# Beginning the six steps of the second layer's factors one pair later in the middle stage

## Chip, cores and metric

The kernel runs on one core of one Trainium2 chip. The metric is device time in microseconds for one launch, the median of three runs. Every number below that has a decimal point is microseconds unless it says otherwise.

## What is computed

The input `x` has 32 sequences of 64 channels and 1024 positions. Two layers follow each other. Each one adds to `x` a product of a convolution stack with a feed-forward matrix:

```python
x = x + ffn0(cond0(x, style))     # then the same with cond1 and ffn1

def _layer(x, style, w, b, mw, mb, typ):          # four of them in a cond
    s = style @ mw.T + mb                         # one scale per sequence and channel
    weight = SCALE * w * s[:, None, :, None]
    demod = lax.rsqrt(jnp.sum(weight * weight, axis=(2, 3)) + EPS)
    weight = weight * demod[:, :, None, None]
    ...                                           # conv: same, up + blur, same, blur + down

# ffn0: scores = x @ Wr.T; top 16 of 64 experts, softmax -> G
#       h = einsum('nd,krd->nkr', x, A); out = 2 * einsum('nkr,kdr->nd', h * G, B)
# ffn1: W[i,o] = scales[o] * nibble[i,o] - zeros[o]; out = x @ W + bias
```

`s`, `demod` and the small matrices made from them and from the convolution weights do not depend on `x`. They are the *factors* of a layer.

## The kernel before

The 128 partitions hold two sequences of 64 channels each, a *pair*; there are `NP = 16` pairs. The program has three stages in time. In the first (0 to 402) every pair goes through the first layer's convolutions and through the product with the scores and `A`; the gated result goes to DRAM (`hgd`). In the middle stage (402 to 628) every pair's result is loaded again (`hg`), transposed on TensorE, and multiplied with `B`; the residual is added and the new `x` goes to DRAM in two forms (`x1d`, `x1e`). In the last stage (628 to 905) every pair goes through the second layer's convolutions and the product with the unpacked weights.

The change lies in the middle stage, in a loop over the pair `p`. One turn of it for a pair from the third on (the first two pairs, `WHOLE`, are simpler and also split `B` into parts):

- `turned_h(p + 1)` transposes the next pair's `hg` with 8 instructions on TensorE into two PSUM banks (`ht`, L1021). VectorE cuts off the high bits (`hh`, L148) and subtracts them (`tlh`, L859), ScalarE copies the high part (`thh`, L863) and scales the low part (`tlh`, L867). GpSimd forms the difference of the two (`tdh`, L875) in `crossed`.
- `layer0b(p)` multiplies: 16 instructions with `thh`, 16 with `tlh` (together called Q here) and 16 with `tdh` (called D), all L895, for two halves of 512 columns with two PSUM banks each. Four banks (`fps`) is all there is, so the next pair's Q begins in a bank that this pair has given up.
- VectorE joins the banks with the residual: L1065 and L1066 for the first half, L1065 and L1066 for the second. Then it makes the differences `dd` (L1108, L1110), beside small edge copies on ScalarE (L1109, L1113) and GpSimd (L1107, L1117), and the SP queue writes them out (L1102, L1104, L1114), loads the next residual (L1047) and the `hg` of two pairs on (L1009).

Beside this the loop makes the second layer's factors. `factors(1, ...)` is a generator of six steps, and one `next(set1)` per pair runs one of them:

1. the loads: `mw`, `mb` on the SP queue (L192, L194), `cw`, `b`, `cu` on ScalarE's queue (L193, L195, L196);
2. squares of the weights on VectorE (L206, L207, L209), copies of the weights on ScalarE (L214 to L220), the styles on TensorE (`sps`, L226, four calls that issue 8 matmuls) with L230 to L233 on VectorE, and a chain on GpSimd that composes a blur with a convolution kernel: two memsets (L238, L239), copies, six additions (L246), copies into `iw` and `cu` (L253, L259);
3. the sums for `demod` on TensorE (`dps`, L263), the root on ScalarE (L271), the reciprocal on VectorE (L272), three transposes (`w2t`, L279) with four copies (L282 to L285), and the first `rows` transpose (L339);
4. about fifteen small instructions on VectorE (L294 to L314) and two on ScalarE;
5. a first constant column on TensorE (`cs`, L325) with two instructions on VectorE (L327, L328);
6. a second one, the second `rows` transpose, and the DMA of the rows to DRAM (`rowd`, L332), from which the tables `tbl` of the last stage are loaded (L563).

Their scratch lies in the array `cv`, where the unsplit `B` was before and where two inputs of the last stage (`cv<-x1e`, L666) and zeroed columns (`clear`, `clear_y`) come after. The order on each engine is made by a scheduler from the order of the program. It lets an instruction move ahead where its data permit; `tc.issue_after(v)` holds what is inside until `v` has been issued. The steps stand behind the pair's `tdh` in this way (`done["td"]`).

Of the kernel before, what the change touches and what calls it, by code (L numbers as in the profile page):

```python
# [62 lines left out]
def adaln_ffn_kernel(ctx: ExitStack, tc: tile.TileContext, t, out: bass.AP):  # L63
# [65 lines left out]
    def yv(n):  # L129
        o = O_Y + (n % 2) * Y  # L130
        return cv[:, o : o + Y]
# [229 lines left out]
    def split_weights(raw, w, ks, into, name, crossed=True):  # L361

        for k in ks:
            ws = block(k, [P, 3, w], F32R, f"{name}{k}")
            for c in range(0, w, H):
                cs = slice(c, min(c + H, w))
                h = high(raw[k][:, cs], f"{name}h{k}_{c}")
                nc.gpsimd.tensor_tensor(ws[:, 1, cs], raw[k][:, cs], h, ALU.subtract)  # L368
                nc.scalar.copy(ws[:, 0, cs], h)  # L369
            into[k] = ws  # L370
            if crossed:
                crossed_weights(into, k)
# [34 lines left out]
    def load_q():  # L407
        qw = wk.tile([P, L], I32, tag="w4", name="qw", bufs=3)
        nc.sync.dma_start(qw, t["qweight"])
        return qw  # L410

    def unpacked(qw):


        wq = []
        aux = block(3, [P, 3, L], F32, "aux")
        for n, v in enumerate(("scales", "zeros", "bias")):
            nc.sync.dma_start(aux[:, n], t[v].partition_broadcast(P))
        for j in range(PACK):
            if j % 3 == 0:  # L420
                w = block(j // 3, [P, 3, QW], F32R, f"wq{j}")
            v = w[:, j % 3]
            nc.gpsimd.memset(v[:, 0:1].bitcast(F32), 1.0)
            nc.gpsimd.memset(v[:, 1:2].bitcast(F32), 0.0)
            for c in range(2):
                nib = wk.tile([P, H], I32, tag="hi", name=f"nib{j}_{c}", bufs=3)
                with tc.issue_after(done["dd"].ins):
                    nc.vector.tensor_scalar(
                        nib,
                        qw[:, c * H : (c + 1) * H],  # L430
                        4 * j,
                        15,
                        ALU.logical_shift_right,
                        ALU.bitwise_and,
                    )
                nc.scalar.copy(v[:, 2 + c * H : 2 + (c + 1) * H], nib)
            wq.append(v)
            if j % 3 == 2:
                yield
        yield wq, aux  # L440
# [204 lines left out]
    def clear(i):  # L645

        for n in range(2):
            if i == 0:
                nc.gpsimd.memset(xdv(n)[:, 0 : L + 3 : L + 2], 0.0)
            nc.gpsimd.memset(fwv(n)[C:, NT * C : 8 * C], 0.0)  # L650

    def clear_y(ys):
        for y in ys:
            nc.gpsimd.memset(y[:, YO : YO + HQ + 1 : HQ], 0.0)
# [216 lines left out]
    def crossed(key):  # L871

        if key in toks and len(toks[key]) == 2:
            td = tokens("td", f"td{key}")
            done["td"] = nc.gpsimd.tensor_tensor(  # L875
                *(v.rearrange("p a b -> p (a b)") for v in (td, *toks[key])), ALU.subtract
            )
            toks[key].append(td)
# [128 lines left out]
    def load_h(p):  # L1007
        hg = wk.tile([P, L], F32, tag="w4", name=f"hg{p}", bufs=3)
        nc.sync.dma_start(hg, hgd[p])  # L1009
        return hg  # L1010

    def turned_h(p, hg):
        whole = p in WHOLE
        key = f"h{p}"
        th = tokens("th", f"th{key}", F32 if whole else F32R)
        toks[key] = [th] if whole else [th, tokens("tl", f"tl{key}")]
        for g in range(2):
            ps = cpst(f"ht{p}_{g}")
            for c in range(4):
                k = 4 * g + c  # L1020
                nc.tensor.transpose(  # L1021
                    ps[:, c * P : (c + 1) * P], hg[:, k * P : (k + 1) * P], ident
                )
            ks = slice(4 * g, 4 * g + 4)

            def d(v):
                return v[:, ks].rearrange("p a b -> p (a b)")

            if whole:
                nc.scalar.copy(d(th), ps)  # L1030
            else:
                split(ps, lambda v: v, d(th), d(toks[key][1]), f"hh{p}_{g}")
        if not whole:
            scaled_low(toks[key][1])
# [3 lines left out]
    def load_residual(p):  # L1038
        if p in WHOLE:
            v = tokens("tl", f"xres{p}", F32).rearrange("p a b -> p (a b)")  # L1040
        elif p < NP - 1:
            v = cv[:, O_Y + Y : O_Y + Y + L]
        elif p < NP:
            v = wk.tile([P, L], F32, tag="w4", name="xres", bufs=3)
        else:
            return
        nc.sync.dma_start(v, t["x"][p])  # L1047
        residual[p] = v
# [137 lines left out]
    def load(k, h=None, rooms=(None, None)):  # L1186
        if k < len(todo):
            i, p = todo[k]
            for h in range(2) if h is None else (h,):
                xin.setdefault(k, []).append(load_x(i, 2 * p + h, rooms[h]))  # L1190

    def tables_of(k):
        if k < len(todo):
            tables(*todo[k])

    def outer_of(k):
        if k < len(todo):
            outer_outputs(*todo[k])

    def begin(k, hs=range(2)):  # L1200
        if k < len(todo):
            i, p = todo[k]
            for h in hs:
                if k < DIRECT:
                    n = 2 * p + h
                    room = xev(n) if k != 1 else room4[:, 2 * XD + 2 * h * HQ :]
                    xin[k][h] = scaled_positions(n, room, *xin[k][h])
                elif i == 0:
                    differences(2 * p + h, *xin[k][h])
                else:  # L1210
                    modulated(2 * p + h)

    def compose(k):
        if k < len(todo):
            gs[k] = composed1(*todo[k])

    def conv(k, h):
        if k < len(todo):
            i, n = todo[k][0], 2 * todo[k][1] + h
            ys.setdefault(k, []).append(first(i, n, yv(n), xin[k][h]))  # L1220
            if i == 1:
                load(k + 1, h)

    def weights(k):
        if k < len(todo):
            fw[k] = composed2(*todo[k], gs.pop(k))

    def later(k, h):
        if k < len(todo):
            i, p = todo[k]  # L1230
            rest(i, 2 * p + h, ys[k][h], fw[k][h])

    def run(g):
        for _ in g:
            pass
# [117 lines left out]
    for p in range(NP):  # L1353
        if p + 1 < NP:
            turned_h(p + 1, hg)
        if p + 2 < NP:
            hg = load_h(p + 2)
        if p == NP - 1:
            clear_y([yv(1)])
            conv(NP, 1)  # L1360
            tables_of(NP + 2)
            outer_of(NP + 1)
            begin(NP + 1)
        if p <= len(WHOLE):
            load_residual(p)
        main = layer0b(p, braw if p in WHOLE else wb)
        next(main)
        if p in WHOLE:
            split_weights(braw, L, range(4 * p, 4 * p + 4), wb, "wb")
        if p == 7:  # L1370
            clear(1)
            clear_y([yv(0)])
        if p == LAST:
            load(NP)
            tables_of(NP)
            set_ends = ends(1, 0, LAST, cv[:, O_FW:])
        if p in (LAST, LAST + 1):
            next(set_ends)
        if p == NP - 2:
            qw = load_q()  # L1380
            tables_of(NP + 1)
            outer_of(NP)
            begin(NP)
            compose(NP)
            conv(NP, 0)
            weights(NP)
        if p == NP - 1:
            unpacking = unpacked(qw)
            compose(NP + 1)
            next(unpacking)  # L1390
            later(NP, 0)
            next(main)
            next(unpacking)
            conv(NP + 1, 0)
            next(main)
            later(NP, 1)
            second = next(unpacking)
            weights(NP + 1)
            next(main)
            conv(NP + 1, 1)  # L1400
        next(main, None)
        if p in (LAST, LAST + 1):
            next(set_ends)
        run(main)
        if p + 1 < NP:
            crossed(f"h{p + 1}")
        if 0 < p < 7:
            with tc.issue_after(done["td"].ins):
                next(set1, None)
        if p == LAST + 1:  # L1410
            run(set_ends)
            for n in range(2):
                nc.gpsimd.memset(fwv(n)[C:, NT * C : 8 * C], 0.0)
# [71 lines left out]
```

## Time and profile before

| quantity | value |
|---|---|
| median of 3 runs | 908.75 (907.94 to 909.59) |
| the profiled execution | 906.81 |
| its span | 904.7 |
| mean granted TensorE clock in it | 0.999 of full speed |
| busy: TensorE, VectorE, GpSimd, ScalarE | 97%, 78%, 52%, 36% of the span |

The span runs from the first to the last instruction in the profile; 2.1 of the profiled execution's time lie outside it. Times of instructions below count from the span's start. Matmul ends are modelled, so the distance from one start to the next is what a group of matmuls costs; a bracket at the end of a row gives the idle time before it and what ended that.

### The profile page before, as it was taken

Reading aid. Unit: us, or ns where it says so; the run is one execution under the profiler, and the core shown is the slowest. Engines: PE = TensorE matmul, PEld = TensorE weight load, DVE = VectorE, ACT = ScalarE, POOL = GpSimd, SP = SyncE. Lnnn points to the kernel's source line nnn. Section 1 sums busy time; section 2 is a strip of 40 time slices with the busy share of each in tenths; the row PEclk is TensorE's granted clock in tenths of the full one; section 3 lists DMA queues with packets and bytes.
Section 4 is the critical chain, followed back from the end, with each engine's and each line's share of the span. In section 5 each row is a group of like instructions: output and inputs, shape, how many; then the busy total and the mean of one; then the engine's idle time right before and its main releaser. Section 6 shows DMA issues by size and latency. Waiting matters only on the chain.

```text
span 904.7 us, 14847 instructions
## 1 busy us (share of the span) xinstructions
PE 876.4 (97%) x5133; PEld 786.2 (87%) x5133; DVE 709.2 (78%) x1450; ACT 328.9 (36%) x717; POOL 468.2 (52%) x605
## 2 busy tenths in 40 slices
PE   5989999999999999999899999999999999999997
PEld 4877789999999999994688888788899999999997
DVE  4565888888888888577986666669998899999986
ACT  6435433333333344333332221247233323333230
POOL 7325654444444444456572222433776767676674
PEclk9999999999999999999999999999999999999999
DMA  8521232222222221354476665556433243333321
GB/s 252 138 72 53 54 95 71 83 79 77 77 77 77 76 77 71 106 175 154 136 227 209 212 195 159 181 191 187 148 111 112 89 130 113 110 109 118 120 65 70
DMA packets 49738, 109.81 MB, mean 121 GB/s; under 512 B 13700, under 2 KB 22400, under 8 KB 49664
## 3 DMA queue, kind: packets, MB, share of 16 engines
q1 hardware_dynamic: 48704, 107.88, 38.9%
q10 hardware_dynamic: 960, 0.99, 0.4%
q8 instruction: 41, 0.67, 0.3%
q14 instruction: 33, 0.27, 0.1%
HBM read 70.97 MB, written 37.88 MB: 120 GB/s over the span
## 4 chain that ended last, share of the span: by engine, by line
PE 77%; DVE 11%; issue 4%; POOL 4%; DMA 2%; ACT 1%; ACTq 0%; SPq 0%; DVEq 0%; POOLq 0%
PE h L895 18%; PE o L895 15%; PE q L1146 12%; PE f L611 6%; PE r L784 6%; PE r L815 5%; PE c L735 5%; PE r L792 3%; PE g L588 3%; PE c L730 2%; DMA x1e<-dd 1%; PE ht L1021 1%; DVE x L1066 1%; POOL wa L368 1%; POOL tdh L875 1%
## 5 line engine op out<-in xcount | busy, mean ns | idle before, releaser
L700 POOL TENSOR_TENSOR cv<-cv 128x256 f32<-128x256 f32 x120 | 77.8, 649 | 123.5 <-DVE su L938 72.7
L697 DVE TENSOR_TENSOR cv<-cv 128x257 f32<-128x257 f32 x120 | 99.8, 863 | 1.2 <-ACT cv L720 1.0
L732 ACT ACTIVATE yt<-c,be,al 128x257 f32<-128x257 f32 x56 | 31.7, 566 | 120.1 <-PE c L730 108.9
L1146 PE MATMUL q<-wq,thx 128*128 128x342 f32 x384 | 73.0, 332 | 1.6 <-ACT thx L853 1.6
L634 POOL TENSOR_TENSOR cv<-cv 128x256 f32<-128x256 f32 x60 | 55.0, 917 | 33.9 <-ACT cv L629 33.9
L1146 PE MATMUL q<-wq,tlx 128*128 128x342 f32 x384 | 72.4, 330 | 0.0
L895 PE MATMUL h<-wa,tdx 128*128 128x352 f32 (+1 forms) x336 | 72.1, 351 | 0.2 <-DVE wa L376 0.2
L800 DVE TENSOR_TENSOR rt<-r,tbl 128x256 f32<-128x256 f32 x60 | 25.0, 417 | 56.3 <-PE r L792 56.3
L611 PE MATMUL f<-gs,iw 128*128 128x128 f32 (+1 forms) x384 | 68.1, 327 | 0.0
L784 PE MATMUL r<-cv 128*128 128x128 f32 x480 | 66.6, 282 | 0.9 <-POOL cv L634 0.5
L611 PEld LDWEIGHTS f<-gs,iw 128*128 128x128 f32 x384 | 61.9, 190 | 5.5
L784 PEld LDWEIGHTS r<-cv 128*128 128x128 f32 x480 | 63.6, 196 | 3.0 <-POOL cv L634 1.7
L875 POOL TENSOR_TENSOR tdx<-thx,tlx 128x1024 fp32r<-128x1024 f32 x14 | 35.5, 2536 | 57.6 <-ACT tlx L867 48.1
L895 PE MATMUL h<-wa,thx 128*128 128x352 f32 (+1 forms) x336 | 64.7, 333 | 0.0
L1146 PEld LDWEIGHTS q<-wq,thx 128*128 128x128 f32 x384 | 60.3, 189 | 3.6 <-ACT thx L853 2.7
L815 PE MATMUL r<-cv 128*128 128x128 f32 x480 | 63.4, 274 | 0.0
L1146 PEld LDWEIGHTS q<-wq,tlx 128*128 128x128 f32 x384 | 61.9, 189 | 0.8
L895 PE MATMUL h<-wa,tlx 128*128 128x352 f32 (+1 forms) x336 | 62.4, 327 | 0.0
L895 PE MATMUL o<-wb,thh 128*128 128x512 f32 x224 | 59.9, 400 | 2.6 <-ACT wb L369 1.6
L626 ACT COPY cv<-f 128x256 f32<-128x256 f32 x64 | 24.0, 375 | 100.8 <-PE f L611 90.3
L895 PEld LDWEIGHTS h<-wa,tdx 128*128 128x128 f32 x336 | 57.1, 188 | 2.3 <-DVE wa L376 0.5
L815 PEld LDWEIGHTS r<-cv 128*128 128x128 f32 x480 | 58.3, 191 | 0.0
(306 smaller groups left out, 2128.6 us busy)
## 6 DMA issues: line engine op xcount, KB each, us to landing
cv<-in_x_dram SPq DMA_DIRECT2D x60, 256.0 KB
cv<-x1e SPq DMA_DIRECT2D x64, 192.5 KB
x1e<-dd SPq DMA_DIRECT2D x16, 514.0 KB
hgd<-hs SPq DMA_DIRECT2D x16, 512.0 KB
hg<-hgd SPq DMA_DIRECT2D x16, 512.0 KB
x1d<-x SPq DMA_DIRECT2D x16, 512.0 KB
xb<-x1d SPq DMA_DIRECT2D x16, 512.0 KB
out_dram<-o SPq DMA_DIRECT2D x15, 512.0 KB
```

The costliest lines, as they stand in the source:

```text
L588: nc.tensor.matmul(ps[:, k * P : (k + 2) * P], tw[:, k].rearrange("p a b -> p (a b)"), r.rearrange("p a b c -> p (a b c)"), start=(k == 0) ...
L611: done["f"] = nc.tensor.matmul(pv[:, n : n + 2 - k], iw[:, e].rearrange("p a b -> p (a b)"), v, start=(m == 0), stop=(m == len(steps) - 1) ...
L634: nc.gpsimd.tensor_tensor(f[:, 4 * P : 6 * P].rearrange("p (a b) -> p a b", b=P), v[:, :, 0], v[:, :, 1], ALU.add,)
L697: nc.vector.tensor_tensor(d[:, k], yo[:, k : k + HQ], yb, ALU.subtract)
L700: nc.gpsimd.tensor_tensor(e[:, :, k], d[:, :, 2 * k : 2 * k + HQ - 2 : 2], d[:, :, 1 : HQ - 1 : 2], ALU.subtract)
L732: nc.scalar.activation(yt, mid, AF.Identity, bias=be0[:, n : n + 1], scale=a)
L735: done["c"] = nc.tensor.matmul(ps, w[:, q], xe[:, o : o + w_], start=True, stop=True)
L784: nc.tensor.matmul(ps[:, j * P : (j + 1) * P], y[:, j + k : j + k + 2 * P - 1 : 2], w(4 + k), start=(k == 0), stop=(k == 1),)
L815: done["r"] = nc.tensor.matmul(ps[:, j * P : (j + 1) * P], y[:, YE + (2 * q + k) * P : YE + (2 * q + k + 1) * P], w(q + 2 * k), start=True ...
L875: done["td"] = nc.gpsimd.tensor_tensor(*(v.rearrange("p a b -> p (a b)") for v in (td, *toks[key])), ALU.subtract)
L895: nc.tensor.matmul(banks[l == 2], toks[key][l][:, order(k)], w[:, cols], start=(k == first and l != 1), stop=(k == last and l in (2, min(n ...
L1146: nc.tensor.matmul(ps, half[:, k], wq[at(k)][:, c * QC : (c + 1) * QC], start=(k == 0 and j == 0), stop=(k == NC - 1 and j == 1),)
```

## The change

`next(set1)` is called in the turns of pairs 2 to 7 where it was called in those of pairs 1 to 6, and the zeroing that shares the scratch is called in pair 8's turn, not in pair 7's. Nothing is added or left out.

```diff
@@ -1367,7 +1367,7 @@
         next(main)
         if p in WHOLE:
             split_weights(braw, L, range(4 * p, 4 * p + 4), wb, "wb")
-        if p == 7:
+        if p == 8:
             clear(1)
             clear_y([yv(0)])
         if p == LAST:
@@ -1404,7 +1404,7 @@
         run(main)
         if p + 1 < NP:
             crossed(f"h{p + 1}")
-        if 0 < p < 7:
+        if 1 < p < 8:
             with tc.issue_after(done["td"].ins):
                 next(set1, None)
         if p == LAST + 1:
```

The order of instructions per engine, set side by side for the two programs, has the same instructions on every engine. Step 1's ten loads, the squares of step 2 on VectorE (L206, L207, L209) and its copies on ScalarE (L214 to L220) stand in the same place in both: the scheduler had already carried them ahead, and the zeroing too, except L654. The rest of the steps stands one pair later on each engine.

## The prediction

> **What bounds the kernel now.** I read the page first, for the bound of the whole.
>
> ```profile
> PE 876.4 (97%) x5133; PEld 786.2 (87%) x5133; DVE 709.2 (78%) x1450; ACT 328.9 (36%) x717; POOL 468.2 (52%) x605
> PE 77%; DVE 11%; issue 4%; POOL 4%; DMA 2%; ACT 1%; ACTq 0%; SPq 0%; DVEq 0%; POOLq 0%
> ```
>
> TensorE is busy for 97% of the span and makes up 77% of the chain that ended last. So a moved instruction counts if it changes how long TensorE idles, or if it leaves a place where TensorE idled anyway. The second view is the timeline of TensorE in the middle stage; pairs 3 and 4 of it are here.
>
> ```profile
> 443.02 3.79 PE L895 MATMUL o<-wb,tdh 128*128 128x512 f32 x16
> 446.65 0.97 PE L226 MATMUL sps<-condT,cv 128*128 128x32 f32 x8
> 447.45 1.07 PE L1021 MATMUL ht<-ident,hg 128*128 128x128 f32 x8
> 449.56 2.08 PE L895 MATMUL o<-wb,thh 128*128 128x512 f32 x8 [1.04 <-DVE cv L1065]
> ...
> 456.94 3.79 PE L895 MATMUL o<-wb,tdh 128*128 128x512 f32 x16
> 460.57 0.97 PE L263 MATMUL dps<-cv 128*128 128x32 f32 x8
> 461.37 0.53 PE L279 MATMUL w2t<-ident,cw 128*128 128x128 f32 x3
> 461.73 1.04 PE L1021 MATMUL ht<-ident,hg 128*128 128x128 f32 x8
> ...
> 470.30 3.79 PE L895 MATMUL o<-wb,tdh 128*128 128x512 f32 x16
> ```
>
> The row to see is the fourth. Pair 3's first product starts after 1.04 of idle, released by VectorE's L1065. Just before it stand `sps`, which is moved, and the transposes. From there to pair 8 TensorE idles once more, for 0.54 before the second `rows` transpose at 501.04. A pair with no step beside it takes 11.79 from one start to the next (511.53 to 523.32).
>
> The third view is VectorE's timeline, to see what L1065 was late for.
>
> ```profile
> 447.46 0.68 DVE L859 TENSOR_TENSOR tlh<-ht,hh 128x512 fp32r<-128x512 f32 x1
> 448.06 0.75 DVE L209 TENSOR_TENSOR cv<-cv 128x256 f32<-128x256 f32 x2
> 448.73 0.68 DVE L1065 SCALAR_TENSOR_TENSOR cv<-o,cv 128x512 f32<-128x512 f32 x1
> 449.45 1.09 DVE L1066 SCALAR_TENSOR_TENSOR x<-o,cv 128x512 f32<-128x512 f32 x1
> 450.37 0.69 DVE L1065 SCALAR_TENSOR_TENSOR cv<-o,cv 128x512 f32<-128x512 f32 x1
> 450.98 0.28 DVE L230 TENSOR_TENSOR cv<-sps,cv 128x128 f32<-128x128 f32 x1
> ```
>
> VectorE works without a gap from 442.35, when it comes out of the last splits of `B`, and reaches pair 2's first join at 448.73. Pair 3 starts 0.14 after that join ends, in the bank that it gives up. What reads `sps` (L230) comes behind. The chain of waits says the same in three pieces: VectorE's L1065 to 449.43, 0.14 of issue, then TensorE for 11.16.
>
> **The change, part by part.** Durations are from the one profiled execution (span 904.7, with 2.1 around it 906.81). That is 1.94 below the median of 908.75, so I work out a difference there and add it to the median.
>
> *What does not move.* Step 1's ten DMAs, L206, L207 and L209 on VectorE and L214 to L220 on ScalarE stand in the same places in both orders. Up to and including both joins of pair 2's first half VectorE's order is the same, and so are SP's and ScalarE's queues and GpSimd's. So L1065 again ends at about 449.42, and pair 3 starts at 449.56.
>
> *`sps` leaves the stall.* It takes 0.80 on TensorE (446.65 to 447.45). Without it the transposes start at 446.65 and pair 3 still starts at 449.56. The idle grows from 1.04 to 1.84 and nothing is gained: 0.00. VectorE's next free slot goes to `hh` (L148, 0.68) in place of L230 (0.28); it delays the second half's L1066 by about 0.4, to about 452.7, and pair 3 needs that bank at 453.31.
>
> *`sps` arrives after pair 3.* Pair 3's products end at 460.57 with no idle behind them, so `sps` is paid there in full: +0.80. The residual load on SP (L1047) and the tail of pair 3's join wait behind L230 by 0.2 to 0.4. Pair 4's products need from pair 3's join only the first half's banks at once, which are free before L230.
>
> *The rest of the steps on TensorE.* `dps` and `w2t` take 1.16 (460.57 to 461.73), the first `rows` 0.16, the two `cs` 0.58 and 0.59, the second `rows` 0.16 with its 0.54 of idle. All were paid in full and are paid in full one pair on, behind the same neighbours: 0.00.
>
> *GpSimd's chain of step 2.* This is the part that could turn into a new wait, because `tdh` queues behind it.
>
> ```profile
> 453.81 0.64 POOL L238 MEMSET cv<- 128x640 f32 x1
> ...
> 455.72 6.87 POOL L246 TENSOR_TENSOR cv<-cv 128x256 f32<-128x256 f32 x6
> ...
> 466.43 2.41 POOL L875 TENSOR_TENSOR tdh<-thh,tlh 128x1024 fp32r<-128x1024 f32 x1
> ```
>
> It runs from 453.81 to 466.02, 12.2 long. Behind it pair 4's `tdh` ended at 468.84, and pair 4's D began at 470.30: 1.46 to spare. In the new order pair 4's `tdh` comes before the chain. It cannot start before pair 3's D ends (460.57), nor before the `dd` memset, which waits for the DMA of pair 2's differences; from issue to release that took 5.4 to 7.0 in later pairs. I take 461.2 to 463.6 for `tdh`, and D of pair 4 starts about 469.4. The chain then runs to about 475.8 and pair 5's `tdh` to about 478.5. D of pair 5 starts at 460.57 + 0.80 + 11.79 (pair 4) + 1.16 (`dps`, `w2t`) + 8.57 (the distance from `ht` to D with a `rows` in between, 461.73 to 470.30) = 482.9. That leaves 4.4 to spare, more than before: 0.00. If the cover were gone, each microsecond past it would be one on TensorE.
>
> A rule of the Trainium skill speaks against this. "SBUF — State Buffer", section "Who interferes with whom", has VectorE instructions with two SBUF inputs block a reading GpSimd instruction outright, and the reverse. Here the six L246 took 732 to 1416 ns beside a full VectorE, and 729 to 1449 at the start of the kernel. By the row the slowing is nothing. By the rule, as an estimate, the four such instructions of two pairs' `dd` (0.68 each) could hold the chain for 2.7. Both are under 4.4, so the sum stays.
>
> *The other queues.* ScalarE takes the root's table load (1.28), the root and seven small copies one pair later; it is busy for about 3 of each pair's 12. On SP two loads of the last stage's input, `rowd` and three `tbl` loads move with their steps. The first `tbl` reader on VectorE (L578) moves by one pair as well and keeps its 7.2 behind the load (509.06 to 516.27). The last readers of the factors begin at pair 12, so one pair of the slack goes unused. L654 is one 0.10 memset behind the chain.
>
> *Sum.* +0.80 in the profiled execution: 907.61. From pair 9 on the orders agree, and everything waits for TensorE, so the shift passes to the end. Against the median: 908.75 + 0.80 = 909.55.
>
> **Rivals.**
>
> *The longer idle costs clock.* "TensorE: Matmul & The Clock Gate", "Part 1: The HAM clock gate", says that an idle window of about 3.4 drops TensorE to half speed until about 3.4 of sustained work. The trace has its kind at the start: eight `sps` matmuls after 6.59 of idle took 1.89, and 0.97 here. In this stage the granted clock is 1.00 through the 1.04 of idle. The place is 446.65 to 449.56, where only 1.07 of transposes would be left in 2.91. It decides from the point where a whole window counts as idle; 1.84 is short of it. If it did, half speed for 3.4 loses 1.7: +2.5, or 911.25. By the row the loss is 0, and I take that.
>
> *`tdh` late behind the chain.* From 4.4 of delay on. With the chain's additions taking twice their 6.87, pair 5 waits 2.5: +3.3, or 912.05. Against it is the equal duration of the additions in both places.
>
> *All of step 2 moves, as the title says.* If L206, L207 and L209 (together 1.9) left the backlog too, L1065 would end 1.9 earlier and the whole idle of 1.84 would go. Then `sps` is paid and 1.84 is gained: -1.04, or 907.71. The two orders speak against it.
>
> *Nothing changes.* If `sps` met some idle in its new place, or pair 3 came 0.8 sooner because it really waited for the transposes: 908.75. The 0.14 between L1065 and the product speaks against it.
>
> **How the numbers follow.** 0.2% is 1.82, about what a measurement of this kernel can tell from no change; the runs shown lie within 0.85 of their median. The exposed `sps` gets 0.76, and its spread puts 0.07 of that above 1.82 and 0.01 below -1.82. Nothing changes: 0.06. All of step 2 moves: 0.06, half of it beyond 0.2%. Clock: 0.06, slower. `tdh` late: 0.06, of which 0.05 slower. So faster 0.01 + 0.03 = 0.04, slower 0.07 + 0.06 + 0.05 = 0.18, and 0.78 between. The range goes from 908.2, somewhat below no change, to 911.3, which takes in the clock; about 0.15 lies outside.
>
> **What would show it.** The profile after should have the transposes right after pair 2's D, about 1.8 of idle before pair 3 with L1065 named, `sps` between pair 3 and the next transposes, no idle before pair 5's D, and `tdh` of pair 5 some 4 ahead of it. I am wrong if pair 3 starts at another distance from pair 2's D than 2.9, if its matmuls take longer than 0.25 each from start to start, or if TensorE shows a wait for `tdh`.

## The result and the profile after

| quantity | before | after |
|---|---|---|
| median | 908.38 (22 runs) | 910.81 (22 runs) |
| ratio | | 1.0023 (95% interval 1.0015 to 1.0031) |
| the profiled execution | 906.81 | 909.73 |
| its span | 904.7 | 907.6 |
| mean granted TensorE clock | 0.9986 (46 other runs, beside the first four experiments; none on record for the 22) | 0.9976 (22 runs) |

The changed kernel is slower by 0.0023 of 908.38, which is 2.1 (1.4 to 2.8). The ratio is the recorded estimate with its interval; it is not the quotient of the two medians, which lie 2.4 apart. The 2.1 is just above the 0.2% (1.82) that the forecast took as measurable, and its interval reaches below that. The forecast was +0.80, a median of 909.55, with a range from 908.2 to 911.3; the measured 910.81 lies within the range, though not for the reason that the range was made for (see below). In the page of after TensorE is again busy for 97% of the span, with less of it on the chain.

```profile
PE 74%; DVE 13%; issue 5%; POOL 4%; DMA 2%; ACT 2%; ACTq 0%; DVEq 0%; SPq 0%; POOLq 0%
```

TensorE has 3 points less of the chain, VectorE 2 more. TensorE's timeline in the middle stage of after shows where.

```profile
439.45 2.85 PE L895 MATMUL o<-wb,thh 128*128 128x512 f32 x8
442.14 2.00 PE L895 MATMUL o<-wb,tlh 128*128 128x512 f32 x8
443.97 3.79 PE L895 MATMUL o<-wb,tdh 128*128 128x512 f32 x16
447.60 1.03 PE L1021 MATMUL ht<-ident,hg 128*128 128x128 f32 x8
449.08 2.08 PE L895 MATMUL o<-wb,thh 128*128 128x512 f32 x8 [0.44 <-DVE cv L1065]
...
456.45 3.79 PE L895 MATMUL o<-wb,tdh 128*128 128x512 f32 x16
460.08 0.97 PE L226 MATMUL sps<-condT,cv 128*128 128x32 f32 x8
460.89 1.07 PE L1021 MATMUL ht<-ident,hg 128*128 128x128 f32 x8
...
476.64 1.30 PE L895 MATMUL o<-wb,tlh 128*128 128x512 f32 x5
479.25 0.23 PE L339 MATMUL rows<-ident,cv 64*32 64x64 f32 x1 [1.31 <-DVE cv L272]
```

Three things are to be seen. `sps` has left the stall and stands behind pair 3's D at 460.08, where it takes 0.81 with nothing idle around it. The stall before pair 3 is 0.44 here and not 1.84, because pair 2's matmuls came late: the group at 439.45 took 2.69 from its start to the next, against 1.83 for eight of the same shape at 442.14 (a stretch of low clock, see below). And the first `rows` transpose waits 1.31 for VectorE's L272. In before it waited for nothing:

```profile
464.47 1.30 PE L895 MATMUL o<-wb,tlh 128*128 128x512 f32 x5
465.70 0.23 PE L339 MATMUL rows<-ident,cv 64*32 64x64 f32 x1
```

What made L272 late stands in two more timelines of after, VectorE's first and then GpSimd's.

```profile
474.61 0.69 DVE L148 TENSOR_SCALAR hh<-ht 128x512 int32<-128x512 int32 x1
475.22 2.51 DVE L1108 TENSOR_TENSOR dd<-x 128x512 f32<-128x512 f32 x1
477.66 0.68 DVE L1110 TENSOR_TENSOR dd<-x 128x510 f32<-128x510 f32 x1
478.26 0.94 DVE L272 RECIPROCAL cv<-cv 128x128 f32<-128x128 f32 x1
```

```profile
464.94 6.90 POOL L246 TENSOR_TENSOR cv<-cv 128x256 f32<-128x256 f32 x6
471.90 1.63 POOL L253 COPY iw<-cv 64x320 f32<-64x320 f32 x4
...
474.78 2.41 POOL L875 TENSOR_TENSOR tdh<-thh,tlh 128x1024 fp32r<-128x1024 f32 x1
```

L1108 subtracts two operands that both lie in SBUF. It took 2.51, and 0.68 in before. It began 0.44 after pair 5's `tdh` on GpSimd and ended 0.54 after it (474.78 + 2.41 = 477.19, against 475.22 + 2.51 = 477.73), so it seems to have done its own 0.6 of work once `tdh` was done. The same three rows of VectorE in before:

```profile
463.05 0.68 DVE L1108 TENSOR_TENSOR dd<-x 128x512 f32<-128x512 f32 x1
463.65 0.94 DVE L1110 TENSOR_TENSOR dd<-x 128x510 f32<-128x510 f32 x1
464.51 0.94 DVE L272 RECIPROCAL cv<-cv 128x128 f32<-128x128 f32 x1
```

There the GpSimd chain still stood in front of pair 4's `tdh` and held it until 466.43, behind all three. In after the chain sits in front of pair 5's `tdh` and ends earlier against VectorE's work, so that `tdh` begins just ahead of L1108. The chain of waits of after carries it:

```profile
475.37 2.29 issue
477.66 0.68 DVE dd L1110
478.33 0.87 DVE cv L272
479.21 0.04 issue
479.25 0.23 PE rows L339
```

The 2.29 called "issue" falls inside L1108: the profile shows no semaphore for it.

The two profiled executions differ by 2.9 in span. Pair 3 starts 0.48 earlier in after; `sps` adds 0.81 and the wait before `rows` 1.31; a wait before `ue` late in the stage, 1.75 for 0.81, adds 0.94; some 0.3 is spread over the rest. The wait before `ue` is taken up again at the end.

From these the theory to test, theory 1: the change costs 0.80 for `sps` plus about 1.3 for the `rows` transpose behind a held L1108. Its rivals: the later steps as such cost something; the longer stall lowers TensorE's clock and that is the second term.

### The profile page after: what moved, and what is told of

Its sections match the earlier page's. It is cut to its first block, busy times and chain, and to the rows that moved or that the text cites. A ratio compares the mean times of both kernels' runs of the same rounds, so it can differ in the third digit from the quotient of the medians.

```text
span 907.6 us, 14848 instructions
## 1 busy us (share of the span) xinstructions
PE 877.8 (97%) x5133; PEld 786.7 (87%) x5133; DVE 707.1 (78%) x1450; ACT 328.3 (36%) x717; POOL 468.8 (52%) x605
## 4 chain that ended last, share of the span: by engine, by line
PE 74%; DVE 13%; issue 5%; POOL 4%; DMA 2%; ACT 2%; ACTq 0%; DVEq 0%; SPq 0%; POOLq 0%
PE h L895 16%; PE o L895 14%; PE q L1146 12%; PE r L784 6%; PE f L611 6%; PE r L815 5%; PE c L735 5%; PE r L792 3%; PE g L588 2%; PE c L730 2%; DMA x1e<-dd 1%; DVE x L1066 1%; DVE cv L697 1%; PE ht L1021 1%; POOL wa L368 1%
## 5 line engine op out<-in xcount | busy, mean ns | idle before, releaser
L697 DVE TENSOR_TENSOR cv<-cv 128x257 f32<-128x257 f32 x120 | 97.3, 843 | 1.2 <-ACT cv L720 1.0
L784 PEld LDWEIGHTS r<-cv 128*128 128x128 f32 x480 | 63.5, 196 | 3.7 <-POOL cv L634 2.0
L1065 DVE SCALAR_TENSOR_TENSOR cv<-o,cv 128x512 f32<-128x512 f32 x26 | 18.0, 691 | 53.0 <-PE o L895 53.0
```

The lines of the kernel that those rows point to most:

```text
L697: nc.vector.tensor_tensor(d[:, k], yo[:, k : k + HQ], yb, ALU.subtract)
L784: nc.tensor.matmul(ps[:, j * P : (j + 1) * P], y[:, j + k : j + k + 2 * P - 1 : 2], w(4 + k), start=(k == 0), stop=(k == 1),)
```

## The experiments

The experiments ran in three groups; the kernel before has a median of 907.38 in the first, 907.17 in the second, 907.80 in the third.

### e1_rows_later: the transpose moved away from L272

```diff
-        last_rows(i, 0, dem[:, 3])
+        if i == 0:
+            last_rows(i, 0, dem[:, 3])
         yield
+        if i == 1:
+            last_rows(i, 0, dem[:, 3])
```

> The changed kernel with the first rows transpose (L339) of the second layer moved from step 3 into step 4, so that it stands one pair later on TensorE; no other engine's order changes except for the copy of its result on ScalarE. Theory 1: of the about 2.1 us that the change costs, 0.80 is sps in a place without idle time and about 1.3 is TensorE's wait in front of that transpose for VectorE's reciprocal (L272). Then the wait goes and the time is the time before plus 0.8 (ratio 1.0009). Rival: the rest of the loss comes from elsewhere (the wait of ue for GpSimd at pair 12, 0.9 us longer in the changed profile, or noise); then the time stays at the time before plus about 2 (ratio 1.0023).

Measured: 908.62, ratio 1.0011 (1.0003 to 1.0019). Its VectorE and TensorE timelines:

```profile
478.69 2.27 DVE L1111 TENSOR_TENSOR dd<-x 128x512 f32<-128x512 f32 x1
```

```profile
450.94 3.62 PE L898 MATMUL o<-wb,thh 128*128 128x512 f32 x8 [1.92 <-DVE cv L1068]
454.36 2.09 PE L898 MATMUL o<-wb,tlh 128*128 128x512 f32 x8
...
489.27 0.23 PE L342 MATMUL rows<-ident,cv 64*32 64x64 f32 x1
```

L1111 is L1108 of after and is still held (2.27), but nothing on TensorE waits for what is behind it. About 1.1 of the 2.1 is gone, though the two intervals touch. The first row shows something else: after 1.92 of idle eight matmuls took 3.42 from start to start where 1.92 is usual (449.08 to 451.00 in after).

### e2_chain_longer: more work on GpSimd

```diff
         with tc.issue_after(done["blur"].ins):
             for hs in halves:
                 nc.gpsimd.tensor_copy(cu[hs, :, hs], cur[hs])
+            if i == 1:
+                for _ in range(3):
+                    nc.gpsimd.memset(t1.rearrange("p a b -> p (a b)"), 0.0)
```

> The changed kernel with three memsets of 128x640 (0.64 us each, on scratch that is no longer read) added at the end of GpSimd's chain of step 2; nothing else changes on any engine. Theory 1: L272 is late because L1108 of pair 4, with two SBUF inputs, is held while GpSimd runs pair 5's tdh (475.22 to 477.66 beside 474.78 to 477.19). The memsets push tdh about 1.9 later, behind L1108; L1108 falls back to 0.7 to 1.0, the wait of the rows transpose to under 0.3, and with 1.9 more work on GpSimd the kernel is about 1.3 FASTER than the changed one: the time before plus 0.8 (ratio 1.0009). Rival: the reciprocal is late for another reason (the root on ScalarE, the DMA that the dd buffer waits for); then L1108 may shorten, but the wait stays at 1.3 and the time at plus 2.1 (1.0023) or more.

Measured: 909.11, ratio 1.0018 (1.0011 to 1.0026). In its profile `tdh` starts at 479.02, behind L1111 (477.65, 0.68) and the reciprocal, and the transpose waits for nothing, as theory 1 has it. The time shows less: the expected 1.0009 was too low, and the interval overlaps that of after, so it is the profile and not the time that speaks for theory 1 here. In the profiled execution the eight matmuls after pair 3's stall again took 3.29 from start to start, some 1.4 too long; whether that explains the rest in all runs is not shown. The three memsets cost nothing that TensorE shows.

### e4_styles_later: `sps` outside the stall, chain where it was

```diff
+        def styles():
+            ...
+        if i == 0:
+            styles()
...
-            squared = nc.gpsimd.tensor_copy(tmp(1), sty2[:, 0, :1])
+            squared = nc.gpsimd.tensor_copy(tmp(1), (sty2 if i == 0 else t0)[:, 0, :1])
...
         yield
+        if i == 1:
+            styles()
+            yield
...
-        if 1 < p < 8:
+        if 0 < p < 8:
```

> The changed kernel with GpSimd's chain of step 2 back at the pair where it was before, and the styles (sps with L230 to L233) where the change has them; the chain's L243 reads another column, so that it need not wait for the styles. The orders of the four other engines are those of the changed kernel. Theory 1: without the chain in front of it pair 5's tdh starts about 1.5 earlier, soon after pair 4's D, and is over but for some 0.5 when L1108 comes: the rows wait falls from 1.3 to between 0 and 0.5, and the time is the time before plus 0.8 to 1.3 (ratio 1.0009 to 1.0014), with sps's 0.80 in it. If the wait has nothing to do with GpSimd it stays at 1.3 and the ratio at 1.0023.

Measured: 908.33, ratio 1.0010 (1.0003 to 1.0018), which is +0.9 for `sps` paid in full and no collision. `tdh` of pair 5 runs from 475.30 to 477.69, and L1108 (L1114 here, at 477.38) meets only its last 0.31 and takes 0.86. It ends 0.55 after `tdh`, as in after, but the transpose at 480.03 waits for nothing.

### e5_copies_later: the collision made in the kernel before

```diff
+        def copies():
             for u, hs in enumerate(halves):
                 ...
+        if i == 0:
+            copies()
         yield
+        if i == 1:
+            copies()
```

> The kernel before with the copies into iw and cu (L253 and L259, 3.3 us on GpSimd) moved from step 2 into step 3, behind pair 4's tdh; nothing else changes on any engine. Theory 1: pair 4's tdh then starts at about 462.9 instead of 466.4, just as VectorE reaches L1108 of pair 3 (463.05). L1108 is held to about 465, the reciprocal comes about 1.7 later, the rows transpose of the kernel before gets the wait that the changed kernel has: 1.3 to 1.8 of idle, time before plus 1.3 to 1.8 (ratio 1.0014 to 1.0020), though GpSimd's critical wait is shorter and nothing was added. Rival: the wait comes from the move by a pair as such; then this kernel shows none and takes the time before (1.0000).

Measured: 910.05, ratio 1.0023 (1.0015 to 1.0031). `sps` is in the stall here, nothing but the chain's copies comes later than in before, and GpSimd does the same work; pair 4's `tdh` merely comes before the copies of the chain. Its three timelines (VectorE, GpSimd, TensorE):

```profile
464.01 2.80 DVE L1114 TENSOR_TENSOR dd<-x 128x512 f32<-128x512 f32 x1
466.74 0.93 DVE L1116 TENSOR_TENSOR dd<-x 128x510 f32<-128x510 f32 x1
467.59 0.94 DVE L278 RECIPROCAL cv<-cv 128x128 f32<-128x128 f32 x1
```

```profile
463.86 2.41 POOL L881 TENSOR_TENSOR tdh<-thh,tlh 128x1024 fp32r<-128x1024 f32 x1
```

```profile
468.59 0.23 PE L345 MATMUL rows<-ident,cv 64*32 64x64 f32 x1 [1.85 <-DVE cv L278]
```

The collision alone puts 1.85 of idle into TensorE, and the kernel is 2.1 (1.4 to 2.8) slower. L1114 ends 0.54 after `tdh` again. Of the 15 runs four lie at 907.48 to 908.50, like before, and eleven at 909.04 to 911.16, so it may not happen in every execution; only one of them was profiled.

### e3_rest_later: steps 1 and 2 put back

```diff
-        if 1 < p < 8:
+        if 0 < p < 8 and p != 3:
```

> Steps 1 and 2 stay where the kernel before has them, `sps` in the stall ahead of pair 3 and GpSimd's chain ahead of pair 4's `tdh`; only steps 3 to 6 come one pair later. If the cost of the change is `sps` outside the stall, the chain that pushes a `tdh` into L1108, and the clock after the longer idle, none of the three is here: ratio 1.0000 (907.4 against 907.4, up to +0.3), idle before pair 3 about 1.0, no wait before the first `rows`, mean clock as before. If it is the later tables and the later steps as such that cost, +1.0 to +2.1 stays: ratio 1.0011 to 1.0023.

Measured: 907.16, ratio 1.0001 (0.9993 to 1.0009). So the loss comes from the place of steps 1 and 2; steps 3 to 6, the tables and the zeroing cost at most 0.8 one pair later, by the interval. The stall in its profile is 1.07. Its L1108 meets the last 0.32 of a `tdh` (472.97 to 475.36), takes 0.87, and ends 0.55 after it.

### e8_no_styles: the kernel before without `sps`

```diff
+        if i == 0:
             spv = mpst(f"sps{i}")[...]
             ...
+        else:
+            spv = mb.unsqueeze(2).to_broadcast([P, NL, B])
```

> The kernel before without the second layer's `sps` matmuls (0.80 on TensorE); L230 reads `mb` twice in their place, so the second layer's styles are not computed. The order of all other instructions is that of before. If the stall hides `sps` and idle costs nothing but itself, the idle ahead of pair 3 grows from 1.04 to 1.84 and the time stays: ratio 1.0000, mean clock as before (0.9987). If the longer idle lowers TensorE's clock, less work takes more time: mean clock about 0.9975, +0.5 to +1.0, ratio 1.0006 to 1.0011. If `sps` was never hidden: -0.80, ratio 0.9991.

In addition L230 is held behind the same join that it follows in before. Measured: 908.02, ratio 1.0007 (0.9998 to 1.0015), mean clock 0.9975. Taking 0.80 of matmuls out of the stall brings nothing, so the stall did hide `sps`: the interval excludes the 0.9991 of "never hidden". TensorE's timeline of the profiled execution:

```profile
436.93 2.80 PE L898 MATMUL o<-wb,tlh 128*128 128x512 f32 x8
439.53 2.82 PE L898 MATMUL o<-wb,thh 128*128 128x512 f32 x8
...
447.63 1.03 PE L1024 MATMUL ht<-ident,hg 128*128 128x128 f32 x8
449.14 2.08 PE L898 MATMUL o<-wb,thh 128*128 128x512 f32 x8 [0.47 <-DVE cv L1068]
```

The stall is 0.47 and not 1.84 because, as in after, the matmuls before it ran slowly. The stall took that in: pair 3 waits for L1065 (L1068 here), and TensorE had lost less than the stall before it.

### e9_filled: the stall filled with matmuls

```diff
+        if p == 2:
+            with tc.issue_after(done["td"].ins):
+                fill = mpst("fill")[:, :B]
+                for _ in range(8):
+                    nc.tensor.matmul(fill, ident, condT, start=True, stop=True)
```

> The changed kernel with the first `rows` transpose in step 4, as in e1_rows_later, and with eight additional matmul calls (`fill`, 128x32, twice as many as `sps` has) in the stall ahead of pair 3; nothing reads what they produce. They take about 1.6 of the 1.84. If the longer idle is what lowers TensorE's clock there, the mean clock comes back to that of before (0.9985), no stretch of clock 0.5 follows pair 3's start at 449.6, and what is left is `sps` outside the stall, +0.80: ratio 1.0009, though TensorE does more work than in e1_rows_later (1.0011, clock 0.9979). If the clock has another cause, both stay as in e1_rows_later. If the stall isn't long enough for the fill: +0.3 on top.

Measured: 909.27, ratio 1.0015 (1.0007 to 1.0024), mean clock 0.9978 (20 runs). The fill took 1.70 (447.40 to 449.10) and left no idle before pair 3. Yet the clock stayed where e1_rows_later had it, so the theory that the longer stall sets the mean clock fails this test. In the profiled execution the slow stretch is at 437 to 441, ahead of the stall. The join that pair 3 needs (L1068 here, at 448.10) had ended by 448.79, and pair 3 started at 449.93: with the stall filled, about 1.0 is paid that the stall took in before.

### after_again: the changed kernel a second time

> The changed kernel itself, on the chip and beside the runs of e9_filled. By the two terms shown so far, 0.80 for `sps` and about 1.3 for the first `rows` transpose behind L1108, and by 0.5 for the clock: +2.1 to +2.6, ratio 1.0023 to 1.0029, mean clock 0.9976. If the collision of `tdh` and L1108 happens in some executions only: ratio near 1.0015, and times in two groups.

Measured: 910.16, ratio 1.0027 (1.0015 to 1.0039), six runs, mean clock 0.9982. In its profile the stall is 1.88, L1108 takes 2.33 from 477.79 while `tdh` runs from 477.17, and `rows` waits 1.13. Here the mean clock is not below the one of before beside it (0.9984), and the loss is as large.

### e6_squares_behind and e7_both_later: the stalls taken away

```diff
+        def squares():
             nc.vector.tensor_tensor(sq, cwr, cwr, ALU.mult)
             ...
+        made = squares() if i == 0 else None
...
-        nc.vector.tensor_tensor(sty2, sty, sty, ALU.mult)
+        v = nc.vector.tensor_tensor(sty2, sty, sty, ALU.mult)
+        if i == 1:
+            with tc.issue_after(v.ins):
+                squares()
```

with the first `rows` transpose as in e1_rows_later. For e7_both_later, in addition:

```diff
+        if i == 1:
+            yield
         last_rows(i, 1, cst)
...
-        if p == 7:
+        if p == 8:
             clear(1)
...
-        if 0 < p < 7:
+        if 0 < p < 8:
```

> The kernel before, but the squares of the second layer (L206, L207, L209, together 1.9 on VectorE) come behind the styles (L230 to L233), so that the joins of pair 2 are not behind them; the first `rows` transpose comes with step 4, since its input is later too. If L1065 is what pair 3 waits for, and it is late by the squares, the 1.04 of idle goes and nothing comes in its place: -1.04, ratio 0.9989. If pair 3 waits for the next thing (transposes, cuts and subtractions on VectorE), less is gained: 0.9993 or more. If the squares only move the wait to pair 4: 1.0000.

> The same, and the second `rows` transpose, its DMA and the zeroing of the scratch one pair later, so that the 0.54 of idle in front of that transpose goes too. If both idles are paid in full: -1.58, ratio 0.9983. If the later tables or the later zeroing are needed at once by another engine: as without it, 0.9989, or slower.

Measured: 906.84, ratio 0.9996 (0.9988 to 1.0003), and 906.96, ratio 0.9992 (0.9984 to 1.0000). TensorE's timeline of e6_squares_behind:

```profile
438.63 3.31 PE L904 MATMUL o<-wb,tlh 128*128 128x512 f32 x8
...
449.36 0.97 PE L229 MATMUL sps<-condT,cv 128*128 128x32 f32 x8
450.16 1.08 PE L1030 MATMUL ht<-ident,hg 128*128 128x128 f32 x8
450.99 2.09 PE L904 MATMUL o<-wb,thh 128*128 128x512 f32 x8
```

The stall is gone, and nothing took its place. In this execution TensorE alone does not show why, because the slow stretch at 438.63 had made it late as well. VectorE does: counted from TensorE's last wait for `wb` (438.29 here, 437.00 in before), pair 2's first join (L1074 here, at 448.26) begins after 9.97 and not after 11.73, so the squares did hold it. The measured gain is less than 1.04, and the slow stretch is one reason: the stall used to take it in, and now it is paid. In the runs with a mean clock of 1.000, which leave no room for such a stretch (half of 3.4 in 905 is 0.002), e6_squares_behind has a mean of 905.75 (5 runs) and before 906.75 (4 runs), which is -1.0; the runs are few, and were picked out afterwards. In e7_both_later the second `rows` transpose waits for nothing, but the tables come late and pair 9 pays for it, as VectorE's and TensorE's timelines show:

```profile
524.24 0.35 DVE L589 SCALAR_TENSOR_TENSOR r<-w3p,al,tbl 128x128 f32<-128x128 f32 x1 [6.70 <-DMA tbl<-rowd]
```

```profile
525.34 2.06 PE L906 MATMUL o<-wb,thh 128*128 128x512 f32 x8 [0.42 <-DVE cv L1076]
```

So 0.54 was traded for 0.42. Neither version is shown to be faster than before beyond doubt.

## Why the prediction was right or wrong

The number fell within the range by luck. The range reached 911.3 to take in a loss of clock behind the longer stall; the wait that came, of the first `rows` transpose, was in neither the sum nor the rivals.

*What does not move; `sps` leaves the stall for nothing.* Right. The orders and the named releaser are as written, and e8_no_styles shows the same from the other side: without `sps` the kernel before is no faster. The forecast idle of 1.84 was seen as 1.88 to 1.94 in four profiles (after_again, e1, e2, e4). In after's own it was 0.44, because of a slow stretch before it. Two of the signs named for being wrong thus appeared: in after pair 3 starts 1.48 from the end of pair 2's D, where 2.9 was forecast (2.92 in after_again), and in e1 and e2 its first matmuls take over 0.4 each. Both come from stretches of low clock and not from another releaser.

*`sps` is paid in full behind pair 3, +0.80.* Right: 0.81 in after (460.08 to 460.89), and +0.9 (0.3 to 1.6) in e4_styles_later, where it is the only term left.

*"The rest of the steps on TensorE ... behind the same neighbours: 0.00".* This is the step that failed. The neighbours on TensorE were the same, but not those of the transpose's input. The first `rows` waits for L272, L272 is behind L1108 and L1110 on VectorE, and L1108 meets pair 5's `tdh` on GpSimd. It cost 1.31 in after, 1.13 in after_again. With it the sum is 0.80 + 1.13 to 1.31 = 1.9 to 2.1, against 2.1 (1.4 to 2.8) measured. Without that wait (e1, e4) +0.9 to +1.0 is left; made alone (e5) the collision is +2.1, with 1.85 of idle.

*GpSimd's chain, 0.00.* `tdh` was in time, as written: it ended at 477.19, 6.7 before pair 5's D at 483.87. But the step asked only whether `tdh` is late for TensorE. An earlier end of the chain (474.4 for a forecast 475.8) put `tdh` in front of L1108, and not behind the reciprocal as in before. The chain started 0.6 earlier than forecast, and it took 11.4 and not 12.2, mostly because its four copies (L253) took 1.63 in after and 2.53 in before. At 12.2 long, as an estimate, it would have let `tdh` begin at about 475.6, behind the start of L1108 (475.22). Being early did the harm; e2_chain_longer, with three memsets more in the chain, has no such wait.

*The rule of "SBUF — State Buffer", "Who interferes with whom".* It was set aside on a reading that cannot decide it. The six L246 took as long beside a busy VectorE as at the start, but every VectorE instruction beside them reads an operand from PSUM (`ht` or `o`), and the rule is about two inputs in SBUF. Where such instructions do meet GpSimd, the trace of before has the rule in both directions. Its L253 stood beside L1108 and L1110 (463.05 to 464.59) and took 2.53; alone, in after, 1.63. And late in the stage L1110 stood beside a `tdh`, as VectorE's and GpSimd's timelines show:

```profile
606.40 2.89 DVE L1110 TENSOR_TENSOR dd<-x 128x510 f32<-128x510 f32 x1
```

```profile
462.66 2.53 POOL L253 COPY iw<-cv 64x320 f32<-64x320 f32 x4
605.88 2.88 POOL L875 TENSOR_TENSOR tdh<-thh,tlh 128x1024 fp32r<-128x1024 f32 x1
```

L1110 takes 2.89 there and ends 0.53 after `tdh`, just as L1108 does in after. So the collision could have been read from before, if the question had been what `tdh` would do to VectorE. By the row alone the term was nothing; by the rule, as an estimate, L1108 is held for up to the length of `tdh` (2.4). TensorE loses the part of that hold that exceeds what L272 had to spare: a hold of 1.8 made a wait of 1.31 in after, one of 2.1 a wait of 1.85 in e5.

*The clock rival.* Partly seen, not settled. Clock 0.5 for some 3.4 right after pair 3's stall is in e1 and e2, and not in e4 or after_again with the same idle. So the prediction's reason, that 1.84 is short of a whole window, did not hold in these two. The mean clock of all runs is lower for after (0.9976) and e8 (0.9975) than for before (0.9986, 0.9983, 0.9984), but e9_filled has 0.9978 without the stall, and after_again 0.9982 with it. What an execution loses at startup or at 437 lies ahead of the first instruction that the change moves (`sps`, 446.65 in before). Within after's runs 0.001 of mean clock goes with about 0.7, so the 0.001 between 0.9986 and 0.9976 could be some 0.7, which would fit beside the 1.9 to 2.1 only within the interval. Whether the change lowers the clock stays open.

*The wait before `ue`* at about 575, in the stage's second half, is 0.81 to 1.11 in seven profiles, before among them, and 1.47 to 2.13 in after, after_again, e4, e5 and e9. The chains of waits trace it to the DMA that writes the differences of the pair before (`x1e<-dd`): it took 5.95 to 6.23 in the seven and 6.59 to 7.25 in the five, and the wait grows with it one for one (5.95 and 0.81 in before, 6.88 and 1.75 in after, 7.25 and 2.13 in e9). The pair before that shows 7.06 in before and 6.13 in after, so this DMA varies without the change too. Whether the change makes it longer at this place is not shown.

*The other rivals.* That all of step 2 moves, and that nothing changes, are excluded by the rows at 447.60 and 460.08. A late `tdh` did not occur.

## What to carry to other kernels

When an instruction is moved on GpSimd, look at what VectorE runs beside each of its neighbours in the new order: here a VectorE subtraction with both operands in SBUF that started just behind a long GpSimd subtraction waited for all of it, and no semaphore in the profile says so. A trace of before may show such a meeting elsewhere in the loop, as an instruction of several times its usual length. Arriving early can cost as much as arriving late. Small work in a stall is free only there (0.80 of `sps` here), and a stall also takes in what goes wrong ahead of it, so removing either needs the trace of several executions.

## What was not expected of the hardware

- TensorE's granted clock fell to 0.50 for about 3.4 after an idle of no more than 1.92. The windows of e1_rows_later (busy times of PE, PEld, DVE, ACT, POOL, then the clock, DMA share and GB/s) show it behind the stall:

```profile
446.00:450.00 4.00, 3.03 (x18) 2.38 (x16) 4.00 (x9) 1.68 (x3) 0.01 (x1) 1.00 0.85 323
450.00:454.00 4.00, 3.06 (x8) 2.43 (x9) 3.96 (x7) 1.44 (x3) 2.14 (x3) 0.64 0.50 140
```

- It fell likewise between 437 and 439 in the profiles of after, e6, e7, e8 and e9, behind two waits of only 0.65 to 0.67 and 0.91 to 0.92; the same two waits (0.64 to 0.67 and 0.91 to 0.92) left it at 1.00 in before, e1, e2, e3, e4, e5 and after_again.
- A held VectorE instruction waits for the rest of the GpSimd instruction and is not slowed by a factor. In the middle stage of the twelve profiles 24 of the `dd` subtractions started during a `tdh` and took 0.79 to 2.90, where 0.68 is their own time; each ended 0.53 to 0.56 after that `tdh`, whether 0.3 of it was left (0.86 and 0.87 in e4 and e3) or nearly all (2.80 in e5).
- GpSimd's `tdh` took 2.40 to 2.41 in the collisions of after, after_again, e1, e5 and e9, as long as without one (2.41 in before). Where L1108 began 0.06 to 0.10 ahead of it, as at 605.81 in before, `tdh` took 2.84 to 2.88. In these meetings the one that started first kept its usual length.
